# A stack of cross-attention layers: scores, subtractions and denominators of the masked layers in another order

## Chip, cores and metric

The kernel runs on one core of one Trainium2 chip. The metric is the device time of one execution in microseconds, the lower the better: the median of the runs shown. All arithmetic is in float32 but for a small bias term in bfloat16.

## What is computed

Four cross-attention layers follow each other on `x` (2048 rows of 256). Keys and values of each come from the same context (1601 rows of 512). Layers 0, 2 and 3 have 16 heads of 64 and add a bias to a few token columns; layer 1 (an RMS norm ahead of it, 16 heads of 16 in groups of 4) is called the grouped layer here. One masked layer, cut to what matters:

```python
q = hidden_states @ Wq; k = encoder_hidden_states @ Wk; v = encoder_hidden_states @ Wv
logits = einsum('bhqd,bhkd->bhqk', q, k) * HEAD_DIM ** (-0.5)
logits = logits + col_bias          # -20 * (1 - mask) in the columns of a few tokens
probs = softmax(logits, axis=-1)
out = einsum('bhqk,bhkd->bhqd', probs, v).reshape(B, HW, HEADS * HEAD_DIM)
return out @ Wo + bo + residual
```

The softmax's maximum over a query's 1601 logits must be known before its exponentials, and the sum of these, the denominator, before the output is projected.

## The kernel before

**Units, chunks, steps.** A masked layer is worked in 8 blocks of 2 heads. Each block is 4 units of 512 queries, so the three masked layers have 96 units; the grouped layer adds 16. A unit goes through the context in 13 chunks of up to 128 keys (the last has 65). A step is one chunk. The main loop (L1266) takes two steps at a time, a *pair*. In one step three units are at work: one at its scores (chunk `ca`), the one before at its exponentials, 18 steps behind, and at its values, 20 steps behind. As 13 is odd, pairs of one unit are (0, 1) to (10, 11) and then (12, chunk 0 of the next unit); those of the next are (1, 2) to (11, 12).

**A chunk.** `masked_scores` (L707) makes the transposed scores, keys on partitions, of two heads in a PSUM buffer "s" of two banks (2 x 512 columns). TensorE does the products, ScalarE copies them to an SBUF tile p (L725), VectorE takes the running maximum `top` over chunks (L728 for chunk 1, L730 after it; chunk 0 has none). `subtract` (L802) adds the negated maxima to p on VectorE, `masked_exp` (L806) takes the exponential on ScalarE and adds it to `sums` on GpSimd (L814), and `values` (L834) multiplies it by the values into the PSUM tile `po`.

**Between scores and exponentials.** After a unit's last chunk `maxima` (L766) transposes `top` into an "s" buffer (8 TensorE transposes, L773), reduces it on VectorE to `ntop` (L774) and sends it through DRAM (`on_all_partitions`, L670: a DMA "cols" and one that spreads it over all partitions). `maxima_spread` (L796) copies the result to the PSUM buffer "b", from which `subtract` reads. That buffer is there once.

**After the values.** `denominators` (L877) transposes `sums` into an "s" buffer (L887), reduces it (L891), takes reciprocals (L892) and spreads them by DMA. `divide` (L911) multiplies by them on GpSimd, `project` (L914) makes the product with `Wo` in an "s" buffer (L920), and VectorE adds it to `xs` (L932, L927 where the bias is added as well).

**PSUM.** Eight banks: two "s" buffers of two banks, "b" of two, one bank `po`, one bank "pm". The "s" buffers take turns: scores of the first and second step of a pair, and a maxima, denominators or project piece where there is one.

**Order.** Instructions of TensorE, ScalarE and VectorE run in the order in which the program writes them (L1320 to L1325 tie each to the one before on its engine). In a pair of masked steps this is: two subtractions, two chunks of scores, two exponentials, two chunks of values, and then *pieces*. `Pieces` (L1069) holds work with a place of its own (`due`: queries of the next unit, denominators, divide, project, each so many steps after the unit's last values) and a queue `fill` of work for the next block (7 pieces of keys and 7 of values, each a slice of 256 keys, in the bank pm). `Pieces.pair` (L1093) runs what is due and then, unless that had a cost, one fill piece; a piece marked `shared` uses pm, and a pair takes only one of those. `Masked.finish` (L974) sets the due steps. A block has 26 pairs: 4 with queries, 4 with denominators, 4 with project and 14 with fill pieces.

Of the kernel before, what the change touches and what calls it, by code (L numbers as in the profile page):

```python
# [10 lines left out]
FP = mybir.dt.float32  # L11
# [3 lines left out]
ALU = mybir.AluOpType  # L15
AX = mybir.AxisListType
PSUM = bass.MemoryType.PSUM

P = 128
QB = 512  # L20
# [6 lines left out]
Piece = namedtuple("Piece", "run cost shared", defaults=(True,))  # L27
# [5 lines left out]

@with_exitstack
def tile_cross_attention_stack(ctx: ExitStack, tc: tile.TileContext, t: dict, out: bass.AP):

# [28 lines left out]
    nc = tc.nc  # L67
    x, cond = t["x"], t["ctx_2048"]
# [5 lines left out]
    NB = S // QB  # L74
    QT = QB // P
    TCH = spans(T, P)
    NT = len(TCH)
# [11 lines left out]
    work = ctx.enter_context(tc.tile_pool(name="work", bufs=2))  # L89
    small = ctx.enter_context(tc.tile_pool(name="small", bufs=2))  # L90
    dram = ctx.enter_context(tc.tile_pool(name="dram", bufs=1, space=bass.MemoryType.DRAM))
    ps_o = ctx.enter_context(tc.tile_pool(name="ps_o", bufs=1, space=PSUM))
    ps_m = ctx.enter_context(tc.tile_pool(name="ps_m", bufs=1, space=PSUM))
    scores_pools = ctx.enter_context(ExitStack())

    ident = const.tile([P, P], FP, name="ident")
    make_identity(nc, ident)
    ones = const.tile([P, P], FP, name="ones")
    nc.vector.memset(ones, 1.0)

    class Scores:
# [16 lines left out]
        def pair(self, shape=(2, QB)):  # L118
            return self.pairs.tile([P, *shape], FP, name="s")
# [18 lines left out]
    psum = Scores()  # L138
# [351 lines left out]
    class Grouped:  # L490
# [5 lines left out]
        name = "L1_xattn_"  # L496
# [168 lines left out]
    def columns(q):  # L665


        return slice(q, QB, QT)

    def on_all_partitions(cols, to):  # L670


        n = cols.shape[1]
        rows = dram.tile([4, P, QT], FP, name="cols", bufs=4)[:n]
        with nc.allow_non_contiguous_dma(reason="1024 values, four at a time"):
            nc.sync.dma_start(out=rows.rearrange("h p q -> p h q"), in_=cols)
        for tile_, heads_ in to:
            src = rows[heads_].rearrange("(o h) p q -> o (h p q)", o=1)
            nc.sync.dma_start(out=tile_, in_=src.to_broadcast(tile_.shape))


    class Unit:
# [191 lines left out]
        def last(self):  # L874
            return self.sub == len(self.layer.SUBS) - 1

        def denominators(self):  # L877

            rden = small.tile([P, len(self.pair), QT], FP, name="rden")
            if self.masked:  # L880
                h = 0
                for pt in psum.heads(False)[0]:
                    of = range(h, h + pt.shape[1])
                    pt = pt.rearrange("p h (q k) -> p h q k", k=P)
                    for h in of:
                        for q in range(QT):
                            nc.tensor.transpose(  # L887
                                pt[:, h - of[0], q, :], self.sums[:, h, columns(q)], ident
                            )
                    h += 1  # L890
                    nc.vector.tensor_reduce(rden[:, of[0] : h, :], pt, AX.X, ALU.add)  # L891
                nc.vector.reciprocal(rden, rden)  # L892
            else:
                nc.vector.reciprocal(rden, self.dens)
            self.by = work.tile([P, QB], FP, name="by", bufs=1)
            on_all_partitions(
                rden,
                [(self.by[self.rows(h)], slice(h, h + 1)) for h in range(len(self.pair))],
            )
# [74 lines left out]
        def finish(self):  # L974

            if self.very_last:
                return [(0, Piece(lambda: self.quarters(of[len(units) - 2]), 2.0))]
            if self.final:

                found = [  # L980
                    (4 if self.b == NB - 2 else 2, Piece(self.denominators, 1.0, False)),
                    (7, Piece(self.divide, 0.0)),
                ]
                if self.b < NB - 2:
                    found.append((10 - 2 * self.b, Piece(self.project_rows, 2.0, False)))
                return found
            if not self.masked:
                return [
                    (1, Piece(self.den_columns, 0.0)), (3, Piece(self.denominators, 0.0)),
                    (6, Piece(self.divide, 0.0)), (8, Piece(self.project, 2.0, False)),  # L990
                ]
            return [
                (2, Piece(self.denominators, 1.0, False)), (5, Piece(self.divide, 0.0)),
                (10, Piece(self.project, 2.0, False)),
            ]


# [4 lines left out]
    for b in range(NB):  # L1002
        nc.scalar.dma_start(
            out=x_rows[b], in_=x[0, ts(b, QB), :].rearrange("(n p) c -> p n c", p=P)
# [5 lines left out]
    units = []  # L1010
# [4 lines left out]
    of = {}  # L1015
# [53 lines left out]
    class Pieces:  # L1069
# [4 lines left out]
        def __init__(self):  # L1074
            self.fill, self.later = deque(), deque()
            self.due = {}
            self.credit = 0.0

        def at(self, step, found):
            for steps, piece in found:  # L1080
                self.due.setdefault(step + steps, []).append(piece)

        def own(self, steps):

            cost, taken = 0.0, False
            for step in steps:
                for piece in self.due.pop(step, ()):
                    piece.run()
                    cost += piece.cost
                    taken |= piece.shared and piece.cost > 0  # L1090
            return cost, taken

        def pair(self, steps, pairs):  # L1093

            cost, taken = self.own(steps)
            many = len(self.fill) + len(self.later) > pairs
            while self.fill and not taken and (many or not cost):
                piece = self.fill.popleft()
                piece.run()
                cost += piece.cost  # L1100
                taken = piece.shared and piece.cost > 0

        def steps(self, steps, share):


            self.credit = max(min(self.credit + share, 2.5), -2.5)
            cost, taken = self.own(steps)
            self.credit -= cost
            while self.fill and not taken and self.credit >= self.fill[0].cost / 2:
                piece = self.fill.popleft()  # L1110
                piece.run()
                self.credit -= piece.cost
                taken = piece.shared and piece.cost > 0
# [13 lines left out]
    pieces = Pieces()  # L1127
# [53 lines left out]
    DELAY, LAG = 5, 2  # L1181
# [81 lines left out]
    def masked(unit):  # L1263
        return unit and unit.masked

    for first in range(0, N + NT + DELAY + LAG + 16, 2):  # L1266
        pair = [Step(first), Step(first + 1)]

        if any(masked(x.scoring) for x in pair):
            if psum.banks:  # L1270
                psum.by_pairs()
        elif pair[0].exping and not pair[0].exping.masked and not psum.banks:
            psum.singly()

        kn, cn = divmod(first + 2 - NT - DELAY, NT)
        ahead = of[kn] if cn == 0 and 0 <= kn < len(units) and of[kn].masked else None
        three = not ahead and not any(masked(x.exping) for x in pair)
        for x in pair:
            x.begin()
        for x in pair:  # L1280
            if masked(x.exping):
                if x.cb == 0 and x is pair[1]:
                    x.exping.maxima_spread()
                x.exping.subtract(x.cb)
        for x in pair:
            if masked(x.scoring):
                x.scoring.masked_scores(x.ca)

        ends = all(masked(x.valuing) for x in pair) and pair[0].cv == NT - 1
        if ends:  # L1290
            pair[0].valuing.values(NT - 1)
        for x in pair:
            if masked(x.exping):
                x.exping.masked_exp(x.cb)
        if ahead:
            ahead.maxima_spread()
        if not ends:
            for x in pair:
                if masked(x.valuing):
                    x.valuing.values(x.cv)  # L1300
        first_unit(first // 2)
        together = masked(pair[0].scoring) and (masked(pair[1].exping) or not pair[1].exping)
        for x in pair:
            x.grouped(three)
            x.end()
            if not together:
                pieces.steps([x.step], x.share())
        if together:
            pieces.pair([first, first + 1], round(pair[0].units_left() * NT / 2))
        if ends:  # L1310
            pair[1].valuing.values(0)
        for x in pair:
            if x.scoring and x.ca == NT - 1:
                x.scoring.maxima()
                if not x.scoring.masked:
                    pieces.at(first + 2, [(0, Piece(x.scoring.maxima_rows, 0.3))])


    last = {}
# [39 lines left out]
```

## Time and profile before

| | us |
|---|---|
| median of 3 runs (lowest, highest) | 4742.91 (4740.15, 4749.87) |
| profiled execution | 4745.24 |
| its span, first to last instruction | 4743.5 |
| TensorE busy | 4596.3 |
| VectorE busy | 3744.2 |
| ScalarE busy | 3226.5 |
| GpSimd busy | 2977.4 |
| masked layer 0, grouped layer, two masked layers (roughly) | 0 to 1310, to 2230, to 4743 |

The costliest groups of the masked layers, by line: sums on GpSimd L814, 2711.0 us; values L849 on TensorE, 1493.5 (some of it in the grouped layer); subtractions L804 on VectorE, 1461.2; scores L713 on TensorE, 1336.7; running maxima L730 on VectorE, 1291.4; exponentials L809, 1254.7, and copies L725, 1234.2, on ScalarE. `ntop` (L774) takes 117.6, `rden` (L891) 115.1, the additions to `xs` (L932) 101.6, each 1.2 us a time, on VectorE.

How to read it: busy time of TensorE is put together from starts and modelled ends, so its products overlap a little in the record and a short wait can be hidden in it. Starts are exact; the distance from one group of products to the next tells what a group costs. An idle time in brackets in the timeline names what ended it. The granted clock was 0.992 on average.

### The profile page before, as it was taken

The numbers are of one execution on the slowest core, as the hardware profiler recorded it, in microseconds if no ns is written. First come the engines' busy times: TensorE is split into PE (matmuls) and PEld (weight loads), VectorE is DVE, ScalarE is ACT, GpSimd is POOL, SyncE is SP. The second block draws the span as 40 slices with busy tenths as digits, with TensorE's granted clock in tenths as the row PEclk, the third lists the DMA queues.
The fourth block names the chain that finished last, engine by engine and source line by source line (L and its number), as shares of the span: only waits on it lengthen the run. The fifth ranks groups of instructions, "written<-read, shape, count | busy, mean of one in ns | idle before, by whom it ended". The sixth has DMA issues, their size and how long they took to land.

```text
span 4743.5 us, 64047 instructions
## 1 busy us (share of the span) xinstructions
PE 4596.3 (97%) x23943; PEld 1914.1 (40%) x23943; DVE 3744.2 (79%) x3768; ACT 3226.5 (68%) x4013; POOL 2977.4 (63%) x1436
## 2 busy tenths in 40 slices
PE   8999999999989999999999999999999999999998
PEld 5444444444433333343444444344444444444433
DVE  5888888888876666653788888888888888888887
ACT  4777777777635555555677777777777777777776
POOL 3777777778730000000677777777777777777787
PEclk9999999999989999999999999999999999999999
DMA  4322323222201010021232232222232223232211
GB/s 150 85 84 79 88 77 86 81 80 78 74 27 38 20 29 21 20 61 39 79 89 84 78 89 78 84 80 82 76 91 73 86 81 85 75 86 77 84 36 39
DMA packets 349892, 337.63 MB, mean 71 GB/s; under 512 B 116421, under 2 KB 305381, under 8 KB 349580
## 3 DMA queue, kind: packets, MB, share of 16 engines
q1 hardware_dynamic: 346310, 328.14, 24.6%
q8 instruction: 189, 3.10, 0.3%
q0 software_dynamic: 1152, 3.28, 0.2%
q10 hardware_dynamic: 2118, 2.10, 0.1%
q14 instruction: 123, 1.01, 0.1%
HBM read 318.49 MB, written 14.69 MB: 70 GB/s over the span
## 4 chain that ended last, share of the span: by engine, by line
PE 87%; DVE 10%; issue 1%; ACT 1%; POOL 0%; DMA 0%; another core or an unknown queue 0%; ACTq 0%; DVEq 0%; POOLq 0%
PE po L849 28%; PE s L713 20%; PE t L744 9%; PE pm L413 7%; PE pm L459 6%; PE pm L483 4%; PE s L920 4%; DVE rden L891 2%; PE s L887 2%; DVE ntop L774 2%; DVE xs L932 2%; PE s L773 2%; DVE top L730 1%; DVE p L804 1%; PE t L819 1%
## 5 line engine op out<-in xcount | busy, mean ns | idle before, releaser
L814 POOL TENSOR_TENSOR sums<-sums,p 128x1024 f32<-128x1024 f32 x1145 | 2711.0, 2368 | 736.8 <-ACT p L809 566.0
L725 ACT COPY p<-s 128x1024 f32<-128x1024 f32 (+1 forms) x1248 | 1234.2, 1014 | 655.3 <-PE s L713 567.6
L804 DVE TENSOR_TENSOR p<-p,b 128x1024 f32<-128x1024 f32 (+1 forms) x1248 | 1461.2, 1210 | 55.5 <-ACT b L799 54.4
L849 PE MATMUL po<-p,v 128*64 128x512 f32 (+3 forms) x8320 | 1493.5, 522 | 4.9 <-ACT p L809 2.6
L730 DVE TENSOR_TENSOR top<-s,top 128x1024 f32<-128x1024 f32 (+1 forms) x1056 | 1291.4, 1223 | 234.1 <-ACT p L725 171.3
L713 PE MATMUL s<-q,kT 64*128 64x512 f32 (+1 forms) x4992 | 1336.7, 629 | 85.9 <-DVE ntop L774 23.2
L809 ACT ACTIVATE p<-p 128x1024 f32<-128x1024 f32 (+1 forms) x1248 | 1254.7, 1057 | 43.8 <-DVE p L804 42.6
L849 PEld LDWEIGHTS po<-p,v 128*64 128x64 f32 (+3 forms) x8320 | 365.7, 125 | 1115.8 <-issue 889.3
L713 PEld LDWEIGHTS s<-q,kT 64*128 64x128 f32 (+1 forms) x4992 | 388.6, 181 | 722.7 <-issue 215.5
L831 ACT ACTIVATE p<-t 128x512 f32<-128x512 f32 (+1 forms) x760 | 413.8, 594 | 297.6 <-PE t L819 256.5
L757 DVE TENSOR_REDUCE row_top<-t 128x1 f32<-128x512 f32 x700 | 451.2, 686 | 196.8 <-PE t L819 165.2
L912 POOL TENSOR_TENSOR oT<-oT,by 128x512 f32<-128x512 f32 x111 | 141.6, 1276 | 656.4 <-DMA by<-cols 336.1
L819 PE MATMUL t<-q,kT 32*128 32x512 f32 (+1 forms) x1520 | 489.1, 643 | 0.0
L744 PE MATMUL t<-kT,q 32*128 32x512 f32 (+1 forms) x1880 | 481.9, 553 | 0.0
L413 PEld LDWEIGHTS pm<-wv,ct 128*128 128x128 f32 (+1 forms) x2600 | 300.4, 187 | 130.4 <-issue 69.0
L413 PE MATMUL pm<-wv,ct 128*128 128x128 f32 (+2 forms) x2600 | 333.3, 281 | 1.7 <-ACT vs L417 0.7
L459 PE MATMUL pm<-ct,wk 128*128 128x256 f32 (+1 forms) x1344 | 316.7, 379 | 5.4 <-ACT ct L284 4.3
L774 DVE TENSOR_REDUCE ntop<-s 128x8 f32<-128x1024 f32 x96 | 117.6, 1225 | 228.4 <-PE s L773 228.4
L459 PEld LDWEIGHTS pm<-ct,wk 128*128 128x128 f32 x1344 | 232.2, 191 | 161.1 <-issue 99.3
L744 PEld LDWEIGHTS t<-kT,q 32*128 32x128 f32 x1880 | 182.5, 185 | 163.1 <-issue 96.7
L799 ACT COPY b<-spread 128x1024 f32<-128x1024 f32 x96 | 97.5, 1015 | 150.9 <-DVE p L804 150.0
L920 PE MATMUL s<-oT,wo 128*128 128x512 f32 x376 | 187.4, 621 | 2.8 <-DVE row_top L757 1.7
(176 smaller groups left out, 2249.8 us busy)
## 6 DMA issues: line engine op xcount, KB each, us to landing
ct<-ctxT SPq DMA_DIRECT2D x288, 512.0 KB
xT<-xT SPq DMA_DIRECT2D x100, 512.0 KB
spread<-cols SPq DMA_DIRECT2D x96, 512.0 KB
by<-cols SPq DMA_DIRECT2D x190, 128.0 KB
xT<-xs SPq DMA_DIRECT2D x16, 512.0 KB
ct<-ctxT SPq DMA_DIRECT2D x48, 130.0 KB
wk<-in_L_xattn_Wk_dram SPq DMA_DIRECT2D x24, 256.0 KB
wv<-in_L_xattn_Wv_dram SPq DMA_DIRECT2D x24, 256.0 KB
```

Of the source, the lines that this page charges most:

```text
L413: nc.tensor.matmul(pv[:md, d, :f], ct(k)[:, d * P : d * P + md], wv[:, k, :], start=(k == 0), stop=(k == NCT - 1),)
L459: nc.tensor.matmul(pk, u.wk[:, k, :], ct(k), start=(k == 0), stop=(k == NCT - 1))
L713: nc.tensor.matmul(s[:m, h, :], self.u.kT[r, a : a + m], self.q[r, :], start=True, stop=(a != TAIL),)
L725: nc.scalar.copy(p[:m], s[:m])
L730: nc.vector.tensor_tensor(self.top[:m], s[:m], self.top[:m], ALU.max)
L744: nc.tensor.matmul(s[:, at : at + n], self.q[r, ts(q, P)], self.u.kT[r, a : a + n], start=True, stop=True,)
L757: nc.vector.tensor_reduce(self.top[:, of, q, k : k + 1], s, AX.X, ALU.max)
L804: nc.vector.tensor_tensor(self.p[c][:m], self.p[c][:m], self.less[:m], ALU.add)
L809: nc.scalar.activation(p[:m], p[:m], AF.Exp)
L814: nc.gpsimd.tensor_tensor(self.sums[:m], self.sums[:m], p[:m], ALU.add)
L819: nc.tensor.matmul(s[:m], self.u.kT[r, a : a + m], self.q[r, :], start=True, stop=True)
L849: nc.tensor.matmul(to, v, p, start=(c == 0 and not part), stop=(c == NT - 1 and part != 0))
```

## The change

It makes five edits, all in the masked layers.

- In a pair, the copies and running maxima of scores now come first on VectorE and ScalarE. The subtractions for the next pair (`ahead`) follow: one after the values, one at the very end of the pair, behind the pieces and `maxima`. Where the next pair's exponentials begin a unit (`new`), both come at the end; where its first is chunk 12 of one unit and its second chunk 0 of the next, chunk 12 is subtracted at the pair's beginning, ahead of the scores.
- `maxima_spread` of a unit runs in the pair ahead of its first exponentials, between that pair's two exponentials, for both alignments.
- If the pair before had a `maxima` or a `project` piece (`scored`), this pair's pieces run in front of its scores and not at its end.
- Denominators: `add_up` multiplies `sums` by ones into pm, which leaves each head's sums on 64 partitions; ScalarE copies them, and two small DMAs bring one row of each head into columns for the reciprocal. `denominators` then has the reciprocal and the DMAs that spread it. The transposes and the reduction go.
- Due steps: `add_up` at 2 (a shared piece of cost 1), `denominators` at 4, `divide` at 6 (5 before), `project` at 10 as before. In the last block they are at 2 or 4, with 2 and 4 added.

```diff
+        def add_up(self):
+            pt = ps_m.tile([P, QB], FP, name="pm")
+            for h in range(2):
+                nc.tensor.matmul(
+                    pt[self.rows(h), :], ones[:, :64], self.sums[:, h, :], start=True, stop=True
+                )
+            self.by = work.tile([P, QB], FP, name="by", bufs=1)
+            nc.scalar.copy(self.by, pt)
+            self.dens = small.tile([P, 2, QT], FP, name="den", bufs=1)
+            with nc.allow_non_contiguous_dma(reason="512 values, four at a time"):
+                for h in range(2):
+                    r = self.rows(h).start
+                    nc.sync.dma_start(
+                        out=self.dens[:, h, :],
+                        in_=self.by[r : r + 1, :].rearrange("o (p q) -> o p q", q=QT),
+                    )
...
             rden = small.tile([P, len(self.pair), QT], FP, name="rden")
-            if self.masked:
-                h = 0
-                for pt in psum.heads(False)[0]:
...
-                    nc.vector.tensor_reduce(rden[:, of[0] : h, :], pt, AX.X, ALU.add)
-                nc.vector.reciprocal(rden, rden)
-            else:
-                nc.vector.reciprocal(rden, self.dens)
-            self.by = work.tile([P, QB], FP, name="by", bufs=1)
+            nc.vector.reciprocal(rden, self.dens)
+            if not self.masked:
+                self.by = work.tile([P, QB], FP, name="by", bufs=1)
...
             return [
-                (2, Piece(self.denominators, 1.0, False)), (5, Piece(self.divide, 0.0)),
-                (10, Piece(self.project, 2.0, False)),
+                (2, Piece(self.add_up, 1.0)), (4, Piece(self.denominators, 0.0)),
+                (6, Piece(self.divide, 0.0)), (10, Piece(self.project, 2.0, False)),
             ]
...
+        ahead = []
+        for step in (first + 2, first + 3):
+            kn, cn = divmod(step - NT - DELAY, NT)
+            unit = of[kn] if 0 <= kn < len(units) else None
+            ahead.append((unit, cn) if masked(unit) else None)
...
-        for x in pair:
-            if masked(x.exping):
-                if x.cb == 0 and x is pair[1]:
-                    x.exping.maxima_spread()
-                x.exping.subtract(x.cb)
+        front = pieces.scored
+        pieces.scored = False
+        taken = pieces.pair(steps, left) if together and front else 0.0
+        ahead = [found for found in ahead if found]
+        new = [unit for unit, c in ahead if c == 0]
+        if new and ahead[0][1]:
+            unit, c = ahead.pop(0)
+            unit.subtract(c)
         for x in pair:
             if masked(x.scoring):
                 x.scoring.masked_scores(x.ca)
+        if masked(pair[0].exping):
+            pair[0].exping.masked_exp(pair[0].cb)
+        for unit in new:
+            unit.maxima_spread()
...
+        if ahead and not new:
+            unit, c = ahead.pop(0)
+            unit.subtract(c)
         for x in pair:
             x.grouped(three)
             x.end()
...
-        if together:
-            pieces.pair([first, first + 1], round(pair[0].units_left() * NT / 2))
+        if together and not taken:
+            pieces.pair(steps, left)
         if ends:
             pair[1].valuing.values(0)
+        if len(ahead) == 2:
+            unit, c = ahead.pop(0)
+            unit.subtract(c)
         for x in pair:
             if x.scoring and x.ca == NT - 1:
                 x.scoring.maxima()
+                pieces.scored |= x.scoring.masked
...
+        for unit, c in ahead:
+            unit.subtract(c)
```

`Pieces.own` also sets `scored` when it ran a piece with a cost that is not shared (a project), takes all that is due up to the pair's steps, and `Pieces.pair` returns the cost.

More of the change, by code (lines that the diff above doesn't have):

```diff
@@ L875, in last @@
             return self.sub == len(self.layer.SUBS) - 1
+        def add_up(self):
[14 more added lines that the diff above has]
+                    )
         def denominators(self):
             rden = small.tile([P, len(self.pair), QT], FP, name="rden")
-            if self.masked:
-                h = 0
-                for pt in psum.heads(False)[0]:
[L883 to L891, printed above, removed]
-                nc.vector.reciprocal(rden, rden)
-            else:
-                nc.vector.reciprocal(rden, self.dens)
-            self.by = work.tile([P, QB], FP, name="by", bufs=1)
+            nc.vector.reciprocal(rden, self.dens)
+            if not self.masked:
+                self.by = work.tile([P, QB], FP, name="by", bufs=1)
             on_all_partitions(
@@ L978, in finish @@
             if self.final:
+                at = 4 if self.b == NB - 2 else 2
                 found = [
-                    (4 if self.b == NB - 2 else 2, Piece(self.denominators, 1.0, False)),
-                    (7, Piece(self.divide, 0.0)),
+                    (at, Piece(self.add_up, 1.0)), (at + 2, Piece(self.denominators, 0.0)),
+                    (at + 4, Piece(self.divide, 0.0)),
                 ]
@@ L1077, in __init__ @@
             self.credit = 0.0
+            self.scored = False
         def at(self, step, found):
@@ L1085, in own @@
             cost, taken = 0.0, False
-            for step in steps:
-                for piece in self.due.pop(step, ()):
+            for step in sorted(step for step in self.due if step <= max(steps)):
+                for piece in self.due.pop(step):
                     piece.run()
                     cost += piece.cost
+                    self.scored |= piece.cost > 0 and not piece.shared
                     taken |= piece.shared and piece.cost > 0
@@ L1101, in pair @@
                 taken = piece.shared and piece.cost > 0
+            return cost
         def steps(self, steps, share):
@@ L1273, in tile_cross_attention_stack @@
             psum.singly()
-        kn, cn = divmod(first + 2 - NT - DELAY, NT)
-        ahead = of[kn] if cn == 0 and 0 <= kn < len(units) and of[kn].masked else None
-        three = not ahead and not any(masked(x.exping) for x in pair)
+        ahead = []
[3 more added lines that the diff above has]
+            ahead.append((unit, cn) if masked(unit) else None)
+        three = not any(ahead) and not any(masked(x.exping) for x in pair)
         for x in pair:
             x.begin()
-        for x in pair:
-            if masked(x.exping):
-                if x.cb == 0 and x is pair[1]:
-                    x.exping.maxima_spread()
-                x.exping.subtract(x.cb)
+        together = masked(pair[0].scoring) and (masked(pair[1].exping) or not pair[1].exping)
+        steps, left = [first, first + 1], 0
+        if together:
+            left = round(pair[0].units_left() * NT / 2)
+        front = pieces.scored
[6 more added lines that the diff above has]
+            unit.subtract(c)
         for x in pair:
@@ L1291, in tile_cross_attention_stack @@
             pair[0].valuing.values(NT - 1)
[L1292 to L1296, printed above, removed]
+        if masked(pair[1].exping):
+            pair[1].exping.masked_exp(pair[1].cb)
         if not ends:
@@ L1301, in tile_cross_attention_stack @@
         first_unit(first // 2)
-        together = masked(pair[0].scoring) and (masked(pair[1].exping) or not pair[1].exping)
+        if ahead and not new:
+            unit, c = ahead.pop(0)
+            unit.subtract(c)
         for x in pair:
```

## The prediction

> **What bounds the kernel now.** I read the page first, then what TensorE waited for, then the timeline of a masked stretch.
>
> ```profile
> PE 4596.3 (97%) x23943; PEld 1914.1 (40%) x23943; DVE 3744.2 (79%) x3768; ACT 3226.5 (68%) x4013; POOL 2977.4 (63%) x1436
> ...
> PE 87%; DVE 10%; issue 1%; ACT 1%; POOL 0%; DMA 0%; another core or an unknown queue 0%; ACTq 0%; DVEq 0%; POOLq 0%
> ```
>
> PE is busy for 97% of the span and is 87% of the chain that ended last, with VectorE (DVE) the only other that counts. So a gain must make PE's sequence shorter or take a wait out of it. Its waits, from the list of waits for PE (total us, times, longest us):
>
> ```profile
> PE s L713 <- DVE ntop L774: 23.2, 90, 0.3
> PE s L713 <- DVE rden L891: 22.9, 91, 0.3
> PE s L713 <- DVE xs L932: 20.9, 81, 0.3
> ```
>
> Three VectorE operations, each about once per unit (96 masked units), hold back a score product. Each frees one of the two score buffers "s". The timeline (start us, length, engine, line) shows what one event really costs:
>
> ```profile
> 2954.86 1.12 PE L773 MATMUL s<-ident,top 128*128 128x128 f32 x8
> 2955.91 1.13 PE L713 MATMUL s<-q,kT 64*128 64x512 f32 x4
> 2956.02 1.23 DVE L774 TENSOR_REDUCE ntop<-s 128x8 f32<-128x1024 f32 x1 [3.35 <-PE s L773]
> 2957.16 2.34 DVE L804 TENSOR_TENSOR p<-p,b 128x1024 f32<-128x1024 f32 x2
> 2957.30 1.13 PE L713 MATMUL s<-q,kT 64*128 64x512 f32 x4 [0.26 <-DVE ntop L774]
> 2958.36 1.94 PE L849 MATMUL po<-p,v 128*64 128x512 f32 x8
> ...
> 2962.21 1.99 PE L713 MATMUL s<-q,kT 64*128 64x512 f32 x8
> ...
> 2963.44 1.93 ACT L725 COPY p<-s 128x1024 f32<-128x1024 f32 x2 [0.75 <-PE s L713]
> 2964.13 1.94 PE L849 MATMUL po<-p,v 128*64 128x512 f32 x8
> 2964.49 2.55 DVE L730 TENSOR_TENSOR top<-s,top 128x1024 f32<-128x1024 f32 x2 [0.27 <-ACT p L725]
> 2965.25 2.01 ACT L809 ACTIVATE p<-p 128x1024 f32<-128x1024 f32 x2
> 2965.99 1.98 PE L920 MATMUL s<-oT,wo 128*128 128x512 f32 x4
> ```
>
> Call a pair's score products A and B, its value products V. Unhindered, A to V takes 1.92 us (2962.21 to 2964.13). After the maxima it takes 2.45 (2955.91 to 2958.36): B may start only when ntop has been reduced out of the buffer that B needs. The event costs 0.53 us, twice the 0.26 that the wait shows, since an interrupted stream pays its start again. A project piece and a denominators piece ahead of A cost the same. Other rows of this timeline: V 1.87 start to start, a fill piece (keys or values of the next block) 1.92 to 1.98, project 1.91, a query piece 1.91, denominators 1.16, maxima 1.05.
>
> One cycle of two units (13 pairs), from one maxima to the next but one, measures 77.8 us (35.4 + 42.4, repeating within 0.1). Its products alone: 13 x 3.79 = 49.3, tail biases 0.5, fill pieces 12.7 (25.5 a block, short last slices counted), queries and projects 7.6, denominators 2.3, maxima 2.1: 74.5. The rest, 3.3, is 6 x 0.53 = 3.2 and a little. **That 3.3 of 77.8 us is all that order can win.**
>
> **The Trainium skill.** "Trainium Kernel Development and Optimization", Performance Expectations, calls matmul busy time a bad metric because matmuls are pipelined. The trace agrees: the 97% hides half of each 0.53, so I count start to start. "PSUM — Partial Sum Buffer", PSUM bank collisions raise a hardware error, says that ScalarE and VectorE may not touch one bank's same quadrant at once, reads included, so that software orders them. Agreed: VectorE's maximum starts at 2964.49, 0.03 after the copy of the same scores should end (2963.44 + 1.01). "TensorE: Matmul & The Clock Gate", Architectural detail, calls the queues of ScalarE and VectorE strict FIFO; no run shows otherwise, and the step that decides rests on it.
>
> **The change, part by part.**
>
> *Denominators by products with ones.* It removes 8 transposes (1.16 us of PE), the rden reduction (1.23 of DVE), and one wait of 0.53. It adds two products of V's shape, half a V pair, 1.87 / 2 = 0.93; a ScalarE copy of 128x512, by L871's row 0.58; two DMAs on SP. On PE it saves 0.23 and the wait per unit. ScalarE, 68% busy, has the copy ready before the next A (about 1.2 us after A starts) needs it. The two DMAs (2 KB each) have no row of the same direction in the masked part; the grouped layer's dens DMAs, of the same shape, have their packets done 1.7 us after issue, about 2 with the receipt. The reciprocal comes a pair later on DVE, behind two maxima and a subtraction: some 6.9 us after the products end, with the DMAs landing at about 3.8. So it waits for nothing; if SP is blocked, DVE stops. SP was already waiting when rden came in all 95 cases (704 us in all), so I price this at 0 and keep 1 us per unit as its upper end. Divide moves from 5 to 6 steps, on POOL, behind sums that run later than its data: 0; project stays at 10.
>
> *Copies and maxima first, subtractions a pair ahead.* Same operations. A score buffer is now free when its maximum ends: A's start + 2.28 (copy, then maximum) + 1.22 = 3.5, B's at A + 4.83 (2964.49 + 2.55 - 2962.21). That is early in an ordinary pair of 5.7. It is late when DVE still has subtractions queued in front.
>
> *A piece in front of scores* after a maxima or a project piece: PE has 1.92 us of other work while DVE empties the buffer (1.33), so B's wait goes. But the front pair then has no piece at its end. V is followed by the next A and B at once, and DVE, idle until the late copies come, falls behind. Take E = 0, the end of the maxima:
> PE: piece 0, A1 1.92, B1 2.88, V1 3.84, A2 5.71, B2 6.67, V2 7.63, then project at 9.50 if nothing waits.
> DVE: ntop to 1.33, a subtraction to 2.4, idle until the copy, maximum A1 at 1.92 + 2.28 = 4.20, maximum B1 to 6.75. B2 needs that buffer: 6.80, so V2 is 0.23 late. Two subtractions to 9.0 (2.34), maximum A2 to 10.15. Project needs A2's buffer: it starts at 10.20. Lost: 0.70 and 0.10 for the restart.
> That is a unit whose maxima end in a pair (12, 0). In the other alignment A1 is the unit's first chunk and has no maximum: maximum B1 ends at 6.34 and B2 is on time, but a third subtraction (chunk 12 of the unit before, put ahead of its spread) stands in front. Subtractions to 9.73, maximum A2 10.87, project 10.92: lost 1.42 + 0.10.
> After project a front piece hides xs in the same way, and its second pair has B late by 0.23 again, in both. The add_up pair behind it, shorter by 1 us, is met with 0.1 us to spare.
> Sum of a cycle: 0.80 + 0.23 + 1.52 + 0.23 = 2.8 against 3.3 before; with 2 x 0.23 from the denominators, **1.0 us less per cycle**.
>
> *The spread of maxima* is now read about 3 us earlier in one alignment: ScalarE comes to it at about 10 (after the first exp). cols goes out at 1.4, spread 2.5 to 3.0 later, its packets end 3.2 to 3.9 after that: at most 8.4, and the receipt. 1 us is left, and a late spread would first delay only an exp that is not due until 16. 0.
>
> **Sum.** Of 96 masked units about 85 run in this rhythm (not the first, the last block, or those at the grouped layer): 42 cycles x 1.0 = 42 us. In the last block, with no fill pieces, VectorE sets the pace (its units take 34 to 41 us although they do less): three rden reductions of 1.23 are 4 us. Total 46. Profiled execution: 4745.2 (span 4743.5); it becomes about 4699. That execution lay 2.3 above the median of the runs, which gives 4697.
>
> **Rivals.**
> *Full cover* (0.20): VectorE isn't late at project, if it catches up on the way. Then all 3.3 + 0.46 = 3.8 per cycle goes: 42 x 3.8 + 4 = 164, 4579. For it: DVE is 79% busy on average. Against: its order is fixed, and the arithmetic above has no gap to put the subtractions into.
> *Nothing* (0.10): stalls 0.5 us longer per unit than I count eat the gain, 4743. Against: each duration in the chain repeats closely.
> *VectorE late, slower* (0.15): one more operation of 1.2 us stands ahead of maximum A2, or the reciprocal waits as long for its DMAs, in each unit. Then a cycle loses 2.4 more: 42 x 1.4 = 59 slower, 4800. It decides from 0.5 us per unit on. For it: add_up leaves 0.1 us. Against: SP had nothing in front of rden.
>
> **Chances.** Forecast 0.55, with its own range 4665 to 4730 (0.4 us per unit either way). The 8-in-10 range takes in full cover and nothing, and leaves out the slower one: 4577 to 4745. About 0.2% (9 us) is what a measurement can tell from no change. Faster: 0.55 x 0.97 + 0.20 = 0.73; the same 0.11; slower 0.16.
>
> **What would show it.** Waits of s L713 for ntop, rden and xs gone from PE; project (L920 before) waiting for top about once per unit, 0.4 to 1.5 us long; A to V 1.92 behind front pieces, about 2.15 in the pair after; DVE busy less by about 115 us, ScalarE more by 55. Wrong if project doesn't wait (full cover), or if the reciprocal or ScalarE's spread copy is what DVE and PE stand behind.

## The result, and the profile after

| | before | after |
|---|---|---|
| median of 4 runs (lowest, highest) | 4746.39 (4740.15, 4751.68) | 4683.84 (4677.08, 4689.89) |
| ratio, with its 95% interval | | 0.9868 (0.9848 to 0.9889) |
| profiled execution (its span) | 4745.24 (4743.5) | 4689.89 (4688.1) |

Faster by 1.3%, against a forecast of 1.0% (4697). The time agrees better than its parts do. The rows of the page after that answer to those of before are engine use and the chain:

```profile
PE 4523.3 (96%) x23563; PEld 1866.2 (40%) x23563; DVE 3614.3 (77%) x3672; ACT 3256.5 (69%) x4108; POOL 2983.9 (64%) x1436
...
PE 77%; POOL 8%; DVE 6%; ACT 5%; issue 3%; DMA 1%; ACTq 0%; SPq 0%; DVEq 0%; POOLq 0%
```

TensorE is still nearly always busy, but its share of the chain has fallen by 10 points. The list of TensorE's waits names where (lines have moved: scores are L715, project L928, the running maximum L732, sums L816):

```profile
PE s L928 <- POOL sums L816: 62.0, 43, 1.4
PE s L928 <- DVE top L732: 21.6, 45, 0.5
...
PE s L715 <- DVE xs L935: 1.3, 3, 0.4
...
PE s L715 <- DVE ntop L776: 1.0, 4, 0.3
...
PE s L715 <- DVE xs L940: 0.3, 1, 0.3
```

The three waits of before (ntop 90 times, rden 91, xs 81) are down to 4, 0 and 1; that for xs where the bias is added, L935 here, went from 8 to 3. In their place project waits once per unit, 0.5 us in one alignment and 1.4 us in the other (the two alignments of pairs, as 13 is odd). The first kind, in the timeline of TensorE after:

```profile
2410.18 1.12 PE L775 MATMUL s<-ident,top 128*128 128x128 f32 x8
2411.13 1.89 PE L461 MATMUL pm<-ct,wk 128*128 128x256 f32 x8
2412.96 1.99 PE L715 MATMUL s<-q,kT 64*128 64x512 f32 x8
2414.87 1.94 PE L851 MATMUL po<-p,v 128*64 128x512 f32 x8
2416.74 2.23 PE L715 MATMUL s<-q,kT 64*128 64x512 f32 x8
2418.90 1.94 PE L851 MATMUL po<-p,v 128*64 128x512 f32 x8
2421.32 1.96 PE L928 MATMUL s<-oT,wo 128*128 128x512 f32 x4 [0.48 <-DVE top L732]
2423.12 1.89 PE L461 MATMUL pm<-ct,wk 128*128 128x256 f32 x8
```

With E, as in the prediction, at the front piece's start (2411.13), project starts at E + 10.19. The prediction had 10.20. The second pair's scores take 2.16 us to its values (2416.74 to 2418.90), as forecast about 2.15. The second kind, all engines, E at 2445.28:

```profile
2447.98 1.26 POOL L920 TENSOR_TENSOR oT<-oT,by 128x512 f32<-128x512 f32 x1
...
2450.94 1.99 PE L715 MATMUL s<-q,kT 64*128 64x512 f32 x8
2451.41 9.70 POOL L816 TENSOR_TENSOR sums<-sums,p 128x1024 f32<-128x1024 f32 x4 [2.17 <-ACT p L811]
2451.49 3.47 DVE L806 TENSOR_TENSOR p<-p,b 128x1024 f32<-128x1024 f32 x3
2452.17 1.93 ACT L727 COPY p<-s 128x1024 f32<-128x1024 f32 x2
2452.86 1.94 PE L851 MATMUL po<-p,v 128*64 128x512 f32 x8
...
2454.88 2.54 DVE L732 TENSOR_TENSOR top<-s,top 128x1024 f32<-128x1024 f32 x2
...
2456.24 1.96 PE L928 MATMUL s<-oT,wo 128*128 128x512 f32 x4 [1.44 <-POOL sums L816]
```

Three subtractions run on VectorE, then maximum A2 from 2454.88 to about 2456.1 (1.22), then project at E + 10.96 (predicted 10.92). The profile names GpSimd's sums as what ended the wait: one of the four ended near 2456.2 as well. Project doesn't read `sums`, and what it reads of GpSimd's, `oT` after divide, was done at 2449.24, 7 us earlier. That speaks for VectorE, and an experiment decides it.

**Where the time went, by stretches.** From the start of one unit's maxima to another's, in the two timelines (masked units numbered from 0):

| stretch | before | after | change |
|---|---|---|---|
| start to unit 30's maxima | 1243.1 | 1212.1 | -31.0 |
| unit 30 to 36, over the grouped layer | 1166.6 | 1198.0 | +31.4 |
| unit 36 to 91 | 2138.4 | 2080.9 | -57.5 |
| unit 91 to the end | 195.4 | 197.0 | +1.6 |

A cycle of two units went from 77.84 to 75.84 us: 2.0 us, where I had forecast 1.0. (Here and below, a cycle is the median time from one maxima to the next but one, from unit 36 on.) And around the grouped layer, where I had forecast nothing, 31 us were lost. The two errors nearly cancel.

### The profile page after: what moved, and what is told of

It reads as the page before. It is cut to its first block, busy times and chain, and to the rows that moved or that the text cites. A ratio compares the mean times of both kernels' runs of the same rounds, so it can differ in the third digit from the quotient of the medians.

```text
span 4688.1 us, 63813 instructions
## 1 busy us (share of the span) xinstructions
PE 4523.3 (96%) x23563; PEld 1866.2 (40%) x23563; DVE 3614.3 (77%) x3672; ACT 3256.5 (69%) x4108; POOL 2983.9 (64%) x1436
## 4 chain that ended last, share of the span: by engine, by line
PE 77%; POOL 8%; DVE 6%; ACT 5%; issue 3%; DMA 1%; ACTq 0%; SPq 0%; DVEq 0%; POOLq 0%
PE po L851 21%; PE s L715 19%; PE t L746 9%; POOL sums L816 7%; PE pm L461 6%; PE pm L415 6%; PE s L928 4%; ACT p L727 3%; PE pm L485 3%; DVE top L732 3%; PE pm L884 2%; DVE p L806 2%; PE s L775 2%; ACT p L811 1%; DVE top L730 1%
## 5 line engine op out<-in xcount | busy, mean ns | idle before, releaser
L816 POOL TENSOR_TENSOR sums<-sums,p 128x1024 f32<-128x1024 f32 x1145 | 2713.5, 2370 | 569.4 <-ACT p L811 507.9
L732 DVE TENSOR_TENSOR top<-s,top 128x1024 f32<-128x1024 f32 (+1 forms) x1056 | 1290.2, 1222 | 306.8 <-ACT p L727 250.7
L727 ACT COPY p<-s 128x1024 f32<-128x1024 f32 (+1 forms) x1248 | 1220.6, 1017 | 370.2 <-PE s L715 295.9
L715 PE MATMUL s<-q,kT 64*128 64x512 f32 (+1 forms) x4992 | 1297.1, 626 | 11.3 <-DVE top L732 6.4
L811 ACT ACTIVATE p<-p 128x1024 f32<-128x1024 f32 (+1 forms) x1248 | 1271.7, 1061 | 44.8 <-DVE p L806 44.4
L715 PEld LDWEIGHTS s<-q,kT 64*128 64x128 f32 (+1 forms) x4992 | 405.9, 182 | 719.1 <-DVE top L732 353.3
L730 DVE TENSOR_TENSOR top<-s,p 128x1024 f32<-128x1024 f32 x96 | 117.6, 1225 | 207.2 <-ACT p L727 207.2
L928 PE MATMUL s<-oT,wo 128*128 128x512 f32 x376 | 187.0, 620 | 89.5 <-POOL sums L816 62.0
L419 ACT COPY v<-pm 128x256 f32<-128x256 f32 (+1 forms) x168 | 60.0, 357 | 243.0 <-PE pm L415 243.0
```

The lines of the kernel that those rows point to most:

```text
L715: nc.tensor.matmul(s[:m, h, :], self.u.kT[r, a : a + m], self.q[r, :], start=True, stop=(a != TAIL),)
L727: nc.scalar.copy(p[:m], s[:m])
L732: nc.vector.tensor_tensor(self.top[:m], s[:m], self.top[:m], ALU.max)
L811: nc.scalar.activation(p[:m], p[:m], AF.Exp)
L816: nc.gpsimd.tensor_tensor(self.sums[:m], self.sums[:m], p[:m], ALU.add)
```

## The experiments

The theory is the prediction's: TensorE is the bound, a wait of its products costs 0.53 us, and in the changed order project waits for VectorE's queue. The first rivals are that the reordering carries the gain, and that project waits for GpSimd, as the profile says.

**Denominators alone**, on the order of before: the kernel before with `add_up`, the new `denominators` and the due steps of the change.

```diff
-                (2, Piece(self.denominators, 1.0, False)), (5, Piece(self.divide, 0.0)),
-                (10, Piece(self.project, 2.0, False)),
+                (2, Piece(self.add_up, 1.0)), (4, Piece(self.denominators, 0.0)),
+                (6, Piece(self.divide, 0.0)), (10, Piece(self.project, 2.0, False)),
```

> Denominators by products alone, on the order of before. Theory (each wait of the products costs 0.53 us per unit, the products are 0.2 to 0.3 shorter than the transposes): a cycle of two units goes from 77.8 to about 76.2 us, the wait for rden is gone and those for ntop and xs stay, the whole gains 42 x 1.6 and a little in the last block: about 4675 us. Rival (the reordering carries the gain): only the shorter products are seen, a cycle of about 77.3, about 4725 us.

Measured: 4672.13 us, ratio 0.9849 (0.9829 to 0.9870), a cycle of 76.13 us. Its waits of TensorE:

```profile
PE s L713 <- DVE ntop L774: 23.2, 90, 0.3
PE s L713 <- DVE xs L938: 20.9, 81, 0.3
```

The wait for rden is gone, the other two are untouched, and this one edit gives as much time as the whole change. In a cycle it gives 1.7 of the 2.0 us; the rest of the change loses elsewhere what it adds there (see the grouped layer below).

**Order alone**: the changed kernel with the denominators of before.

```diff
-                (2, Piece(self.add_up, 1.0)), (4, Piece(self.denominators, 0.0)),
-                (6, Piece(self.divide, 0.0)), (10, Piece(self.project, 2.0, False)),
+                (2, Piece(self.denominators, 1.0, False)), (5, Piece(self.divide, 0.0)),
+                (10, Piece(self.project, 2.0, False)),
```

> The order and the pieces in front alone; denominators stay transposes with a reduction, and count as a piece that calls for one in front. Theory (front pieces hide ntop, rden and xs, but put VectorE behind at project): a cycle of 76.5 to 77.3 us, and the 30 us lost around the grouped layer remain, so between 4715 and 4745 us. Rival (the reordering carries the gain): about 4695 us.

Measured: 4730.92 us, ratio 0.9966 (0.9952 to 0.9980), a cycle of 77.28 us. The rival falls: the order gives a quarter of the gain. It takes the waits for ntop and xs away, and that for rden in one alignment (91 times before, 43 here), and puts new ones in their place. One part of the expectation missed: around the grouped layer 12 us were lost, not 30.

**No pieces in front.**

```diff
-        front = pieces.scored
+        front = False
```

> The change without pieces in front of scores. Theory: the waits for ntop and xs are back, four of 0.53 us in a cycle, while project no longer waits and B is no longer late, so a cycle of about 76.0 us, as good as with them; the stretches around the grouped layer lose less, so 4665 to 4685 us. Rival (front pieces are worth their hidden waits): a cycle of 77.5 to 78 us, 4750 us or more.

Measured: 4668.22 us, ratio 0.9832 (0.9816 to 0.9849), a cycle of 75.94 us. Project's waits for `top` are gone from the list, and those for ntop (90 times, 23.2 us) and xs (81 times, 20.9 us) are back. In a cycle the front pieces win 0.1 us; over the whole kernel they cost 16. Most of that is not their order but the clock: the two profiled executions differ by 21.2 us and by 30.6 us of time at half speed, half of which is 15.3 (how this is counted stands below, with the grouped layer).

**Chunk 12 later.** The block that subtracts chunk 12 is moved from ahead of the pair's scores to behind them.

```diff
-        if new and ahead[0][1]:
-            unit, c = ahead.pop(0)
-            unit.subtract(c)
         for x in pair:
             if masked(x.scoring):
                 x.scoring.masked_scores(x.ca)
+        if new and ahead[0][1]:
+            unit, c = ahead.pop(0)
+            unit.subtract(c)
```

> The change with the subtraction of chunk 12 behind the scores of its pair instead of ahead of them. Theory (project waits for the score maximum that stands behind three subtractions on VectorE): the wait of project in that alignment falls from 1.4 to about 0.3 us, a cycle from 75.85 to 74.7, the whole to about 4638 us. Rival (project waits for GpSimd's sums, as the record names them): the wait stays at 1.4 and the time at 4684 us.

Measured: 4631.91 us, ratio 0.9757 (0.9741 to 0.9773), a cycle of 74.72 us. Project's wait in this kernel, both alignments together:

```profile
PE s L928 <- DVE top L732: 35.1, 88, 0.5
```

The waits of 1.4 us for "POOL sums" are gone, though nothing was done to GpSimd's work: they were VectorE's. The profile had named the engine whose event came at the same moment. Its chain follows the same names: GpSimd's share is 8% in the change and 3% here, so the 8% did not measure what GpSimd cost.

**A subtraction in VectorE's idle time.** In a front pair behind a maxima, VectorE idles between the last subtraction and the score copy. One of the next pair's subtractions goes there.

```diff
+        if taken and topped and ahead and not new:
+            unit, c = ahead.pop(0)
+            unit.subtract(c)
         for x in pair:
             if masked(x.scoring):
```

> The change with one of the next pair's two subtractions moved ahead of the scores in the pair whose pieces run in front behind a maxima, where VectorE idles 1.7 us for the score copy. Theory (project waits for what stands on VectorE): project's waits of 0.5 and 1.4 us become 0 and about 0.3, a cycle of 75.85 becomes about 74.1, the whole about 4612 us. Rival (project waits for GpSimd's sums or its own operand): both waits stay, 4684 us.

Measured: 4612.17 us, ratio 0.9710 (0.9692 to 0.9728), a cycle of 74.19 us. Project waits for `top` in one alignment alone now, 0.3 us a time:

```profile
PE s L928 <- DVE top L732: 13.8, 44, 0.4
```

**No front piece behind a flush.** At the start of unit 36's block three pieces were left over in the change (two before) and were run at once; the front piece then waited for its context slice. In the timeline of TensorE after:

```profile
2365.37 1.09 PE L415 MATMUL pm<-wv,ct 128*65 128x128 f32 x8 [0.46 <-ACT v L419]
...
2367.94 3.40 PE L461 MATMUL pm<-ct,wk 128*128 128x256 f32 x8 [1.48 <-DMA ct<-ctxT]
2371.27 2.19 PE L715 MATMUL s<-q,kT 64*128 64x512 f32 x8
```

```diff
             self.release()
+            if self.fill:
+                self.scored = False
             while self.fill:
```

> The change without a front piece in a pair that has just flushed left-over fill pieces (the second masked block after the grouped layer). Theory (there the front piece stands in front of the scores waiting for a context slice whose load had only just been issued): the unit interval of 50.7 us goes back to about 45, cycles stay at 75.85, the whole about 4678 us. Rival (the loss around the grouped layer comes from the granted clock alone): that interval keeps its length, 4684 us.

Measured: 4674.07 us, ratio 0.9848 (0.9832 to 0.9865). The interval of 50.7 us (unit 35's maxima to unit 36's) is 46.0 and cycles stay at 75.85. Of the 4.7 us, about 1.7 is clock: the clock record has 3.41 us at half speed there (from 2368.3, right behind the wait; the piece takes 3.40 us, 1.89 elsewhere), and none without the front piece. The wait of 1.48 us is half of the other 3. The whole gained more than this interval, 9.8 us, but the rest is not shown to be the edit's: the two profiled executions also differ by 13.7 us of half-speed time earlier, within the grouped layer.

**All three edits together.**

> The change with all three edits: chunk 12 subtracted behind the scores, one subtraction in VectorE's idle time behind a maxima, no front piece behind a flush. Theory: no wait of project is left (2.2 us of a cycle), a cycle of about 73.6 us, the whole about 4585 us. Rival (VectorE is busy enough that another wait takes its place): a cycle of 74.7 or more, 4630 us or more.

Measured: 4591.60 us, ratio 0.9678 (0.9661 to 0.9695), a cycle of 73.84 us: 3.2% below before, 2.0% below the change (4591.60 / 4683.84). No wait of project for `top` is left in the list. Engine use and chain:

```profile
PE 4504.6 (98%) x23563; PEld 1861.2 (41%) x23563; DVE 3621.9 (79%) x3672; ACT 3250.7 (71%) x4108; POOL 2983.9 (65%) x1436
...
PE 94%; DVE 2%; ACT 2%; POOL 1%; issue 1%; DMA 0%; SPq 0%; ACTq 0%; another core or an unknown queue 0%; POOLq 0%; DVEq 0%
```

TensorE is 94% of the chain here, 77% in the change.

**The same with divide a step later** (7 for 6).

> As the one with all three edits, and divide a step later (7), so that GpSimd comes to it a pair later in one alignment. Theory (GpSimd's waits of 1 to 3 us for the by DMA are hidden, since its sums run ahead of their need): no difference to it beyond 0.1%. Rival (those waits hold back the score copies, which need tiles that the sums free): 10 to 20 us faster than it.

Measured: 4596.31 us, ratio 0.9680 (0.9663 to 0.9697), the same cycle. As a trial of the rival it is weak, since it did not take GpSimd's waits for the by DMA away: from unit 36 to 91 there are 17 of 16 us together without the edit and 19 of 18 us with it. That they cost nothing in the rhythm is read from the traces: no score copy waits for `sums` there, in either.

**The stretch over the grouped layer** was given no kernel of its own, since ten traces have it. The granted clock in it, before and after (start and end, length, busy time of TensorE, of its weight loads, VectorE, ScalarE and GpSimd with the number of instructions, then granted clock, DMA share, GB/s):

```profile
1243.00:2410.00 1167.00, 1137.09 (x8513) 446.94 (x8513) 754.30 (x1060) 660.95 (x1072) 214.42 (x128) 0.98 0.16 43
```

```profile
1212.00:2410.00 1198.00, 1161.87 (x8486) 449.24 (x8486) 746.63 (x1054) 663.29 (x1077) 213.76 (x126) 0.95 0.15 42
```

The clock records of the traces know full and half speed only. Half-speed time in the stretch is 58.0 us before and 119.5 after. Take half of it off, and 1166.6 becomes 1137.6 and 1198.0 becomes 1138.3. The eight experiments give 1131 to 1141 when treated so, with 75 to 113 us at half speed. So by this estimate nearly all of the 31 us is clock, not more work; TensorE's busy time, in which slower products count, grew by 24.8 of them. The size of the loss belongs in part to the execution: the change's four runs took 4677.08 us at a granted clock of 0.988 to 4689.89 at 0.985, and the profiled one is the slowest.

The Trainium skill, "TensorE: Matmul & The Clock Gate", Part 1, "What's actually happening", has the array's clock set by a monitor of its activity. The traces agree in that the clock halves for multiples of 3.41 us, mostly where TensorE waits for others. The page's section on HAM oscillation speaks of idle gaps over about 3.4 us; here less was enough. Cut into windows of 3.41 us along the clock's own changes, the ten traces have 143 windows at full clock in which TensorE was idle for 1.5 us or more (by the modelled ends of its products), and 90 of them were followed at once by half clock. Of the 5810 windows with less than 0.5 us idle, 27 were.

Why half clock came twice as long in the change is only partly shown. The left-over pieces at unit 36's block are one place. While unit 31 was at its scores, GpSimd waited 3.0 us for the by DMA (to 1218.1), and score copies then waited for its sums; that is read from the trace, and divide a step later did not remove it (2.8 us in that run). And a window alike in TensorE's share had opposite ends in the last block of the grouped layer, in the change and in before:

```profile
2160.10:2163.51 3.41, 1.90 (x14) 0.35 (x12) 2.45 (x2) 1.89 (x3) 0.00 (x0) 1.00 0.00 0
2163.51:2177.17 13.66, 13.66 (x50) 3.60 (x48) 1.23 (x1) 5.48 (x6) 0.00 (x0) 0.50 0.00 0
```

```profile
2193.77:2197.18 3.41, 1.90 (x10) 0.60 (x10) 1.23 (x1) 2.39 (x3) 0.00 (x0) 1.00 0.00 0
2197.18:2210.83 13.65, 12.08 (x82) 3.67 (x84) 3.83 (x4) 8.25 (x9) 0.00 (x0) 1.00 0.05 2
```

TensorE was busy for 1.90 of 3.41 us in both, and only one was followed by half clock; that stays open.

## Why the prediction was right

**The bound and its price: right.** TensorE's sequence sets the rhythm, and an interrupted product costs 0.53 us. The forecasts for denominators alone (76.2, measured 76.13) and no front pieces (76.0, measured 75.94) were worked out with that price.

**The new wait: right, in place, order and size.** Project waits for maximum A2 behind VectorE's subtractions at E + 10.20 and 10.92 by the working, 10.19 and 10.96 by the trace. Moving one subtraction takes 1.12 us from a cycle, where one subtraction is 1.2. The delays left in the changed cycle add up to 2.84 us by starts, 2.8 forecast. Full cover and the slower rival both fall with that: VectorE neither caught up nor fell further behind.

**Right at cost nothing:** the reciprocal waited for its DMA once in 95, 3.9 us; the spread's copy waited 11.6 us in all for its DMA; moving divide changed nothing in the rhythm. VectorE lost the reductions of 115.1 us and ScalarE took on copies of 56.7, as forecast (115 and 55).

**Mis-sized: "1.0 us less per cycle".** It measured 2.0. The waits were counted well; the step that was mis-sized is the rest of the sum, the distances from one group of products to the next, which were carried over from the old neighbours. They can be read from starts, here at `add_up` and above in the timeline of the first wait:

```profile
2430.88 1.94 PE L851 MATMUL po<-p,v 128*64 128x512 f32 x8
2432.65 1.03 PE L884 MATMUL pm<-sums,ones 128*64 128x512 f32 x4
2433.60 2.06 PE L715 MATMUL s<-q,kT 64*128 64x512 f32 x8
```

Maxima take 0.95 to a piece and 1.05 to scores; project 1.80 and 1.91; a piece to scores 1.82 when it follows maxima or project, 1.92 when it follows values; values take 1.77 to `add_up` and 1.87 to others. Four front pieces and two `add_up` in a cycle, in round figures: 4 x (0.10 + 0.10) + 2 x 0.10 = 1.0. Steady stretches then give 88 us in place of 42.

**Wrong: "not those at the grouped layer", priced at nothing.** 31 us were lost there, by the estimate above nearly all to the clock, which the sum left out without a reason. The last block gave +1.6 in place of -4; its granted clock was 0.95 over the last 193 us, 0.99 before.

So 42 + 4 forecast, and 88 - 31 - 2 = 55 in the profiled executions. That the time came out so close is in part luck: two errors of opposite sign. The forecast of the mechanism needed none.

## What to carry to other kernels

When a wait is hidden by moving work ahead of it, write the in-order queues of all engines out for the next two periods: the work moved ahead makes another engine idle now and late afterwards, and the cure can be one operation put into that idle time. Change what makes the wait before changing where it falls: here the shorter product that needs no score buffer was worth three times the reordering in a cycle (1.7 and 0.6 us), four times in the whole. And check that the engine named as releaser was not merely simultaneous.

## What had not been expected of the hardware

- The cost of a group of products depends on its neighbours by 0.10 us: 1.05 us from maxima to scores and 0.95 to a piece of full height.
- Half clock came behind windows in which TensorE was idle well under 3.4 us: after 1.5 us or more in a window of 3.41 it came 90 times of 143 in these traces, after less than 0.5 us 27 times of 5810.
